# Issuing a four-layer graph kernel in the exact order of its own list schedule

## The chip, the cores and the metric

The kernel runs on one core of a Trainium2 chip. The metric is the device time of one execution in microseconds (us). Each number of a run below is the median of its timed executions.

The engines are called PE (TensorE, matrix products and transposes), ACT (ScalarE), DVE (VectorE), POOL (GpSimd) and SP (which issues the DMAs). L462 means line 462 of the kernel.

## The reference, cut to what matters

The input is x of 64 x 256 x 128 and one adjacency of 256 x 256, all in fp32. Four residual layers follow one another, each closed by a layer norm.

```python
x = _layernorm(x + gated_gnn(x, adj, 5 steps))      # layer 0
x = _layernorm(x + softmax_adjacency_gnn(x, adj))   # layer 1
x = _layernorm(x + gat_then_gin(x, adj))            # layer 2: two layer norms inside
x = _layernorm(x + chebyshev(adj, x, order 3))      # layer 3

# one step of layer 0 (u3, sigmoids, tanh: three gates in a row)
m  = adj @ h;  av = [m, m];  u3 = h @ u3_w.T + u3_b
z  = sigmoid(av @ w3_w.T + w3_b + u3)
r  = sigmoid(av @ w4_w.T + w4_b + u3)
hv = tanh(av @ w5_w.T + w5_b + (r * h @ u5_w.T + u5_b))
h  = (1 - z) * h + z * hv
```

The 64 batches are independent of one another. The kernel works on them as 32 pairs and keeps several pairs in flight, so that one pair's matmuls fill the time in which another pair waits.

## The kernel before

The kernel is written as a list of operations with what each reads and writes. A list scheduler in the kernel's own Python gives each operation a start time from assumed durations, chooses between ACT and DVE where both can do the work, and assigns the buffers. It then emits the instructions in order of these start times.

```python
SEEN = {"PE": 0.3, "ACT": 0.15, "DVE": 0.15, "POOL": 0.2, "SP": 3.3}   # handover to another engine
DUE, LAST_DUE, LAST = 50.0, 10.0, 7                                   # pace of the pairs, and of the last ones
...
    def order(self, tiles):
        ...
                for engine, us, fn in op.ways:
                    start = max(op.ready, held, engines[engine])
                    key = (start + (us if len(op.ways) > 1 else 0.0), self.due(op.pair) - op.rest, op.number)
                    if best is None or key < best[0]:
                        best = key, start, op, engine, us, fn
        ...
            out.append((start, op.number, op, fn))
        ...
        return [(op, fn) for _, _, op, fn in sorted(out, key=lambda x: x[:2])]
```

The layer norm: its statistics are on DVE, two small steps on POOL add epsilon and raise to the power of -0.5, a small DVE step (L462) makes the offset, and four instructions on ACT (L473) or DVE (L468) normalise.

```python
        dve(1.75, fn, [y], [st, s])                        # L455: 4 bn_stats (L452) and 4 bn_aggr (L454)
        ...
        pool(1.04, lambda: nc.gpsimd.tensor_tensor(rs(), rs(), neg_half.ap, op=ALU.pow), [s, neg_half], [s])   # L460
        nmr = lambda: s.at(32)[:, 12:16]
        dve(0.16, lambda: nc.vector.scalar_tensor_tensor(nmr(), mv()[:, :, 0], -1.0, rs(), op0=ALU.mult, op1=ALU.mult), [s], [s])   # L462
        ...
        S.add([("ACT", 1.85, by_act), ("DVE", 1.45, by_dve)], [y, s], [o])          # L475: L473 or L468
```

Layer 0, which is most of the matrix work, has three tanhs (ACT: L491, L497, L505) and four gate products (DVE: L493, L507, L508, L510) between its matmuls. In all but the last four pairs its state is turned by a DVE transpose (L421), a DMA to DRAM (L422) and four DMAs back (L426); this is so both before and after the change. PSUM tiles are copied out by ACT (L192) or DVE (L193).

The end of the kernel hands the list to the framework. The framework has a scheduler of its own, and before the change that scheduler was free to set the order of each engine's instructions.

```python
    for op, fn in S.order(tiles):
        for v, ap in op.tiles.items():
            v.ap = ap
        fn()
```

Of the kernel before, what the change touches and what calls it, by code (L numbers as in the profile page):

```python
# [165 lines left out]
def kernel(ctx: ExitStack, tc: tile.TileContext, x, xT, adj, adjT, mats, cols, rows, out):  # L166
# [6 lines left out]
    S = Schedule(n_pairs)  # L173
# [485 lines left out]
    tiles = {}  # L659
    for cls, (n, count) in CLASSES.items():  # L660
        where = {"PS": psum, "D": dram, "E": dram}.get(cls, shared)
        tiles[cls] = [where.tile([1, n] if cls == "D" else [P, n], F32, name=f"{cls.lower()}{k}") for k in range(count)]
    for op, fn in S.order(tiles):
        for v, ap in op.tiles.items():
            v.ap = ap
        fn()


# [39 lines left out]
```

## Time and profile before

The time on which the prediction was made was 1814.8 us, the median of three runs.

The prediction below shows the busy sums, the waits, PE's gaps, the time at half clock and how many instructions stood out of the list's order. Two more views help to see where in the execution the time was lost. First the windows of the kernel before. The columns are the window, its length, the busy us of PE, PE's weight loads, DVE, ACT and POOL with their instructions, the granted clock (as a share of full speed), the DMA share and GB/s.

```profile
0.00:1500.00 1500.00, 1417.83 (x5885) 1001.60 (x5886) 1010.86 (x2750) 710.22 (x1478) 341.19 (x397) 0.99 0.20 61
1500.00:1809.00 309.00, 267.54 (x1333) 204.45 (x1331) 200.49 (x712) 149.99 (x342) 99.17 (x122) 0.96 0.05 14
```

PE lacked 82 us of the first 1500 us, where many pairs are in flight. This is not a shortage of other pairs' work, and no other engine was full there: DVE was busy for two thirds of it. Next, the shares of the span in the chain of work that ended last.

```profile
PE 18%; DVE 11%; POOL 6%; ACT 3%; issue 2%; DMA 1%; SPq 0%; POOLq 0%; DVEq 0%; ACTq 0%
```

The shares sum to 41%: the profile could follow this chain back only to about 1049 us. In the part that it did follow, PE is less than half of the way, and small work on DVE and POOL takes nearly as much.

### The profile page before, as it was taken

How to read it: one execution, taken by the hardware profiler on the slowest of the kernel's cores; microseconds unless marked ns; L12 is line 12 of the kernel's file. 1: busy time of each engine (PE TensorE's matmuls, PEld its weight loads, DVE VectorE, ACT ScalarE, POOL GpSimd, SP SyncE). 2: the span in 40 equal slices, each digit the busy share in tenths (PEclk: the TensorE clock that was granted, in tenths of full speed). 3: DMA queues.
4: the chain of work that ended last, by engine and by line, in shares of the span. 5: the costliest groups of instructions: out<-in, count | busy, mean ns of one | idle time of the engine just before them, and what ended most of it. 6: DMA issues, size and time to landing. Idle time of an engine off the chain costs nothing. (4 is left out here: it accounts for less than half of the span.)

```text
span 1808.5 us, 22671 instructions
## 1 busy us (share of the span) xinstructions
PE 1685.4 (93%) x7216; PEld 1206.1 (67%) x7216; DVE 1211.3 (67%) x3461; ACT 860.2 (48%) x1820; POOL 440.4 (24%) x519
## 2 busy tenths in 40 slices
PE   8999999998999999999999999999999999998886
PEld 5666676667667667676675766667667666666765
DVE  5667666766766765767758576667657755767764
ACT  3444543455455453555444444435544634444653
POOL 0002221113322222212222113221322031215352
PEclk9999999999999999999999999999999999999899
DMA  6211112221111212211212121212211100000000
GB/s 191 92 60 59 41 53 65 87 65 35 59 41 52 84 37 63 88 47 48 70 36 73 44 77 42 70 36 70 76 35 48 59 24 7 7 18 7 12 24 24
DMA packets 129623, 96.13 MB, mean 53 GB/s; under 512 B 11872, under 2 KB 110688, under 8 KB 129504
## 3 DMA queue, kind: packets, MB, share of 16 engines
q1 hardware_dynamic: 129504, 94.69, 16.9%
q8 instruction: 57, 0.93, 0.2%
q14 instruction: 62, 0.51, 0.1%
HBM read 56.83 MB, written 37.81 MB: 52 GB/s over the span
## 5 line engine op out<-in xcount | busy, mean ns | idle before, releaser
L192 ACT COPY a<-ps 128x512 f32<-128x512 f32 (+1 forms) x422 | 215.3, 520 | 292.4 <-PE ps L438 189.5
L457 POOL TENSOR_SCALAR s<-s 128x4 f32<-128x4 f32 x160 | 53.5, 334 | 948.6 <-DVE s L454 853.6
L438 PEld LDWEIGHTS ps<-aT,a 128*128 128x128 f32 x1024 | 248.9, 309 | 33.6 <-issue 18.5
L438 PE MATMUL ps<-aT,a 128*128 128x256 f32 x1024 | 266.4, 401 | 1.4 <-ACT a L192 1.0
L460 POOL TENSOR_TENSOR s<-s,neg_half 128x4 f32<-128x4 f32 x192 | 202.1, 1053 | 15.8
L452 DVE BATCH_NORM_STATS2 s<-a 128x6 f32<-128x128 f32 x640 | 141.5, 281 | 60.5 <-ACT a L192 58.7
L505 ACT ACTIVATE a<-ps,bzrh 128x512 f32<-128x512 f32 x160 | 109.0, 682 | 142.9 <-PE ps L503 140.6
L462 DVE SCALAR_TENSOR_TENSOR s<-s 128x4 f32<-128x4 f32 x192 | 38.5, 201 | 206.3 <-POOL s L460 206.1
L491 ACT ACTIVATE a<-ps,bzrh 128x512 f32<-128x512 f32 x160 | 108.9, 682 | 136.9 <-PE ps L488 135.9
L503 PE MATMUL ps<-a,u5h 128*128 128x512 f32 x320 | 165.9, 600 | 8.0 <-DVE a L493 8.0
L495 PE MATMUL ps<-a,w 128*128 128x512 f32 x320 | 164.0, 603 | 9.4 <-ACT a L491 9.3
L488 PE MATMUL ps<-a,w 128*128 128x512 f32 x320 | 164.6, 597 | 5.6 <-ACT a L192 5.6
L502 PE MATMUL ps<-a,w 128*128 128x512 f32 x320 | 164.6, 596 | 0.0
L529 PEld LDWEIGHTS ps<-W,a 128*128 128x128 f32 x1024 | 128.1, 194 | 51.3 <-ACT a L192 19.9
L529 PE MATMUL ps<-W,a 128*128 128x128 f32 x1024 | 135.1, 280 | 24.1 <-ACT a L192 13.2
L473 ACT ACTIVATE x<-a,s 128x128 f32<-128x128 f32 x248 | 107.9, 485 | 97.3 <-DVE s L462 97.3
L507 DVE TENSOR_TENSOR a<-a,a 128x512 f32<-128x512 f32 x128 | 93.3, 729 | 72.1 <-ACT a L505 72.0
L493 DVE SCALAR_TENSOR_TENSOR a<-a,a 128x512 f32<-128x512 f32 x128 | 89.7, 703 | 64.7 <-ACT a L491 64.1
L487 PE MATMUL ps<-a,W 128*128 128x512 f32 x256 | 131.1, 594 | 1.4 <-DVE h L555 1.3
L508 DVE SCALAR_TENSOR_TENSOR a<-a,a 128x512 f32<-128x512 f32 x160 | 120.0, 752 | 18.1 <-ACT a L497 15.5
L497 ACT ACTIVATE a<-ps,bzrh 128x512 f32<-128x512 f32 x160 | 108.8, 682 | 47.9 <-PE ps L495 46.9
L438 PE MATMUL ps<-aT,x 128*128 128x256 f32 x512 | 128.4, 392 | 3.3 <-ACT x L473 3.2
(147 smaller groups left out, 2816.1 us busy)
## 6 DMA issues: line engine op xcount, KB each, us to landing
e<-a SPq DMA_DIRECT2D x112, 256.0 KB
a<-e SPq DMA_DIRECT2D x448, 64.0 KB
t<-xT_in SPq DMA_DIRECT2D x32, 256.0 KB
x<-x_in SPq DMA_DIRECT2D x32, 256.0 KB
a<-d SPq DMA_DIRECT2D x32, 256.0 KB
y_out<-a SPq DMA_DIRECT2D x32, 256.0 KB
W<-mats_in SPq DMA_DIRECT2D x1, 832.0 KB
W<-mats_in SPq DMA_DIRECT2D x1, 512.0 KB
```

Of the source, the lines that this page charges most:

```text
L192: S.add([("ACT", us_act, lambda: nc.scalar.copy(o(), i())), ("DVE", us_dve, lambda: nc.vector.tensor_copy(o(), i()))], r, w)
L438: nc.tensor.matmul(t.at(2, N)[:, b, :], i.tile(2 * b + j), right.ap[:, j, :], start=(j == 0), stop=(j == 1))
L452: nc.vector.bn_stats(st.at(4, 6)[:, c, :], tokens(y)[:, c, :])
L460: pool(1.04, lambda: nc.gpsimd.tensor_tensor(rs(), rs(), neg_half.ap, op=ALU.pow), [s, neg_half], [s])
L487: nc.tensor.matmul(t.at(512), mat("u3"), hT.at(512), start=True, stop=False)
L488: nc.tensor.matmul(t.at(512), w345.ap[:, 1, :], mT.at(512), start=False, stop=True)
L495: pe(mm(512), lambda t=t, mT=mT: nc.tensor.matmul(t.at(512), w345.ap[:, 0, :], mT.at(512), start=False, stop=True, skip_group_check=True), ...
L502: nc.tensor.matmul(t.at(512), w345.ap[:, 2, :], mT.at(512), start=True, stop=False)
L503: nc.tensor.matmul(t.at(512), u5h.ap, r.at(512), start=False, stop=True)
L505: act(0.69, lambda t=t, hv=hv: nc.scalar.activation(hv.at(512), t.at(512), AF.Tanh, bias=bzrh.ap[:, 2:3]), [t, bzrh], [hv])
L508: dve(0.74, lambda hv=hv, z=z: nc.vector.scalar_tensor_tensor(hv.at(512), z.at(512), 1.0, hv.at(512), op0=ALU.add, op1=ALU.mult), [hv, z], ...
L529: nc.tensor.matmul(tokens(t)[:, c, :], tokens(i)[:, c, :], w(), start=(k == 0), stop=(k == len(lefts) - 1))
```

## The change

The intent is to keep the list's order, which the kernel had computed with the handovers and buffers in view, through to the chip. The whole diff:

```diff
-    for op, fn in S.order(tiles):
-        for v, ap in op.tiles.items():
-            v.ap = ap
-        fn()
+    with tc.manual_schedule():
+        for op, fn in S.order(tiles):
+            for v, ap in op.tiles.items():
+                v.ap = ap
+            fn()
```

Inside this block every engine issues in program order. The instructions and the buffers are the same in both builds.

## The prediction

> **What bounds the kernel now.** I read the page's first two parts, the windows, the waits of TensorE, then those of ScalarE (ACT) and VectorE (DVE), and last the timeline around single gaps. The page says who is full:
>
> ```profile
> PE 1685.4 (93%) x7216; PEld 1206.1 (67%) x7216; DVE 1211.3 (67%) x3461; ACT 860.2 (48%) x1820; POOL 440.4 (24%) x519
> PEclk9999999999999999999999999999999999999899
> ```
>
> TensorE is the bound: 93% busy, with 1808.5 - 1685.4 = 123 us in which no matmul runs, 7 us of that after the last matmul. DVE and ACT have a third and a half of the span to spare, so their sums do not bound; only when they do things can. The windows, in four stretches of 400 us and one of 209, put PE at 382.6, 377.0, 373.3, 383.3 and 169.2 us busy: 84 us of the idle time lie before 1600 us, where many pairs of batches are in flight and there is plenty of other work, and about 40 in the tail, where few pairs are left. What PE waited for, the largest:
>
> ```profile
> PE ps L642 <- ACT a L192: 14.5, 7, 3.3
> PE ps L529 <- ACT a L192: 13.2, 10, 3.8
> PE ps L402 <- DVE a L510: 13.1, 6, 4.2
> PE ps L495 <- ACT a L491: 9.3, 10, 2.0
> PE ps L529 <- ACT a L612: 8.2, 8, 1.7
> PE ps L503 <- DVE a L493: 8.0, 5, 2.8
> ```
>
> So PE waits for short results, a PSUM copy (L192), a tanh (L491), a gate product (L493), from engines that are half idle. Why were these late? The columns are total us, times, longest us:
>
> ```profile
> DVE s L462 <- POOL s L460: 206.1, 178, 4.3
> ...
> ACT x L473 <- DVE s L462: 97.3, 49, 6.3
> ACT a L603 <- POOL a L602: 78.2, 24, 5.9
> ACT a L473 <- DVE s L462: 71.0, 37, 6.6
> ...
> ACT b L579 <- DVE s L571: 48.5, 24, 4.9
> ```
>
> These are layer-norm and softmax steps that stand in ACT's and DVE's queues before their inputs exist, most of them waiting for the 1.05 us power on POOL (L460, 192 times). One case from the timeline (start, duration, what, idle before and its releaser), ACT, then PE:
>
> ```profile
> 1142.49 0.37 ACT L192 COPY a<-ps 128x256 f32<-128x256 f32 x1 [1.04 <-PE ps L635]
> 1147.75 0.51 ACT L579 ACTIVATE b<-b,h 128x256 f32<-128x256 f32 x1 [4.89 <-DVE s L571]
> 1148.17 0.35 ACT L192 COPY a<-ps 128x256 f32<-128x256 f32 x1
> ...
> 1148.57 0.67 PE L642 MATMUL ps<-a,a2T 128*128 128x256 f32 x1 [3.02 <-ACT a L192]
> ```
>
> The L635 products were done by about 1144.2, but ACT sat 4.89 us at L579 with the copy behind it, and PE stood still 3.02 us. It then paid again; the windows of this gap and of what follows it (third column from the right: granted clock):
>
> ```profile
> 1145.50:1148.60 3.10, 0.08 (x2) 0.03 (x1) 2.18 (x6) 0.85 (x3) 0.89 (x1) 1.00 0.22 63
> 1148.70:1152.10 3.40, 3.40 (x9) 2.69 (x10) 2.90 (x12) 2.78 (x10) 0.00 (x0) 0.51 0.21 78
> ```
>
> For 3.4 us after the gap PE ran at half clock. The trace has 16 such stretches; by their lengths they cost 31 us (the mean granted clock, 0.983, gives the same: 0.017 x 1808.5). Of 19 gaps of 2 us or more, 13 are followed by one within 4 us.
>
> [...]
>
> **The change part by part.** No instruction is added or taken away: the builds have the same 4092 matmuls, 3461 DVE, 512 POOL and 726 DMA instructions, and buffers are given out by the list before emission, so they are the same too. Only the place of each instruction in its engine's queue changes. In the old build 43 of 4092 PE instructions stand out of the list's order, against 841 of 3461 on DVE and 472 of 1689 on ACT (least number to move to restore it); in the new build none do. The move of each instruction, counted as the trace duration of the work placed ahead of it on its engine:
> - ACT: the normalisations L473 go later in 373 of 472 cases, 3.9 us on average; L603 in 23 of 25, 3.8 us. What feeds PE goes earlier: the three tanhs in 333 of 480 cases, by some 1.9 us, the copies L192 in 250 of 423, by 1.35 us.
> - DVE: L468 (normalisation) goes later in 240 of 296, L565 in 56 of 64 (3.2 us), L571 in 27 of 32 (3.0 us); L508, L510, L588 and the statistics go earlier, by 0.7, 0.8, 2.2 and 1.4 us.
> - PE and SP keep nearly all places, and 142 of 192 POOL powers keep theirs.
>
> In the case above the old queue has the first L579 ahead of three L192 copies; the new one has it behind them.
>
> The cost, step by step. (1) I paired the trace with the built program and followed each PE gap (95 over 0.03 us, 115.8 us, the 6.1 us of the first load included) back to the first instruction that started over 0.15 us after its inputs, and looked at what ran ahead of it there. In 80 gaps, 94.4 us, something that ran ahead stands behind it in the new order: 58.8 us on ACT, 35.6 on DVE; 77 of the 94 lie before 1600 us. I let 80% go, -75 us. (2) New waits: a fixed order still misses where the list's durations are off. Its POOL, DVE and ACT durations are close to the trace (power 1.04 against 1.053, transpose 1.11 against 1.114, four statistics with aggregation 1.75 against 4 x 0.281 + 4 x 0.158 = 1.756), its transposes through PE less so. I choose +15 us. (3) PE idle thus goes from 116 to some 56 us. Long gaps should fall at least as much: half clock from 31 to some 15 us, -16 us. (4) Steps between matmuls that are over 0.1 us above the median of their kind sum to 171 us; gaps and clock account for 116 + 31 less the 2 us of half clock after the last matmul, leaving some 25 us of refill after a stall. Fewer stalls: -10 us. Sum -75 + 15 - 16 - 10 = -86, so 1814.8 - 86 = 1729; I round to 1727.
>
> A floor for comparison: the median steps between matmuls sum to 1607.6 us; with 6 us ahead of the first matmul, 7 us after the last and the 6 us between profile and timing, 1627. The range stays well above it.
>
> **The rivals.** (a) *The stall moves, it does not go.* Strict order makes ACT and DVE issue whole groups: the statistics of one tile hold DVE 1.75 us where the old build could slip a gate product in between. If the list misjudges DMA or PE, the head of a queue blocks as before. For it: 5 of 64 L565 go earlier and 42 of 160 L493 later. Against: L493 is on average earlier, and a turned state lands a median 7.8 us before PE first reads it, with only 0.4 us of PE waits put down to those transfers. It would give 1775 to 1810. (b) *The tail decides.* After 1600 us the chain runs through POOL powers and DVE reductions, and order cannot shorten a dependence. Then only the part before 1600 us is won, about 60 us with its clock: 1755. (c) *Everything the list plans comes true*: idle some 25 us and hardly any half clock, 1690. (d) *DMA or the two half-idle engines become the bound*: the sums, 1211 us DVE and 17% of the DMA queues, speak against it; no time goes to it.
>
> **Range and chances.** Rival (c) is the low end, a weak form of (a) the high end: 1690 to 1770. Faster by over 2% needs under 1778.5, that is only 36 us of the 86. Since 80 of 95 gaps have their blocker moved, I give that 0.92; within 2% 0.06; slower 0.02, for an order that blocks in ways which the old trace cannot show.
>
> **What would show it right or wrong.** Right: PE busy share of 96% or more; the waits of L473, L603 and L579 on ACT (97.3 + 71.0 + 78.2 + 48.5 = 295 us) at least halved, that of L462 on POOL well down; PE waits on L192, L491 and L493 down to a third; granted clock above 0.99; PE, DVE and ACT busy sums unchanged within 2%, apart from PE's at half clock. Wrong, if PE's idle time stays above 90 us with new lines at the head of its waits (DMA a<-e, L588 or L421), or if the ACT waits fall and the span does not, which would make the tail or PE's own pitch the bound.

## The result

The changed kernel took 1691.38 us (1689.64 to 1693.74, four runs). In the same rounds the kernel before took 1815.44 us (1813.13 to 1819.7, four runs). The ratio is 0.9315, with a 95% interval from 0.9294 to 0.9336. A ratio here is the mean time of one kernel's runs over that of the other's of the same rounds, so it is not quite the ratio of the medians. The change is 124 us faster; the time predicted was 1727 and the range 1690 to 1770, so the result lies 1.4 us inside its lower end.

The busy sums of the kernel after:

```profile
PE 1646.8 (97%) x7216; PEld 1198.1 (71%) x7216; DVE 1257.4 (74%) x3461; ACT 875.1 (52%) x1820; POOL 451.8 (27%) x519
```

PE's idle time fell from 123 to 1689.5 - 1646.8 = 43 us. Its busy time also fell by 38.6 us with the same instructions: some 19 us of this is less time at half clock, and the rest, as the account below suggests, is fewer slow matmuls around a stall. Now the windows of the kernel after, in the same columns as above (the second one ends with the span, at 1689.5 us).

```profile
0.00:1500.00 1500.00, 1489.92 (x6350) 1069.12 (x6351) 1121.72 (x2970) 772.31 (x1569) 373.36 (x424) 1.00 0.20 62
1500.00:1809.00 309.00, 156.84 (x869) 129.00 (x866) 135.68 (x491) 102.83 (x251) 78.44 (x95) 0.96 0.04 11
```

Of the first 1500 us PE now lacks 10, and 8.3 of those are the wait for the first load. PE got through 6350 instead of 5885 instructions in that time. After 1500 us it lacks 189.5 - 156.8 = 33 us: what is left of the idle time is in the tail.

The waits of PE after (total us, times, longest us), largest first:

```profile
PE ps L438 <- DMA aT<-adjT_in: 8.3, 1, 8.3
PE ps L305 <- ACT b L582: 6.8, 4, 6.1
PE ps L438 <- ACT x L473: 3.3, 2, 3.1
PE ps L529 <- ACT a L612: 2.6, 3, 0.9
```

The copies, tanhs and gate products that led this list before are gone from its head. The second line is new: L305, the transposes of the softmax, waited 1.1 us for L582 before. The account of the prediction comes back to it. The waits on L192 copies fell from 41.7 to 5.2 us in all, those on L491 from 9.3 to 0.8, and those on L493 from 8.0 to nothing. The waits of ACT and DVE after, which answer to the lines of L462, L473, L603 and L579 before:

```profile
ACT a L192 <- PE ps L438: 225.0, 196, 10.1
...
DVE s L462 <- POOL s L460: 43.5, 52, 2.4
...
ACT b L579 <- DVE s L571: 9.7, 13, 1.7
...
ACT a L603 <- POOL a L602: 5.1, 9, 1.2
...
ACT a L473 <- DVE s L462: 3.0, 2, 1.7
ACT x L473 <- DVE s L462: 3.0, 2, 2.2
```

ACT is still idle for half of the span, but now it waits almost only for PE, that is, for the bound: 763 of the 804 us of its waits, against 619 of 939 us before. The waits of L473 (both tiles), L603 and L579 together went from 295 to 3.0 + 3.0 + 5.1 + 9.7 = 21 us. The chain that ended last, after:

```profile
PE 93%; DVE 3%; ACT 1%; POOL 1%; issue 1%; DMA 0%; SPq 0%; POOLq 0%; DVEq 0%; ACTq 0%
```

The prediction showed a case in which ACT stood 4.89 us at an L579 with a ready copy behind it. The same place in the list comes at about 1064 us of the kernel after. First ACT in its timeline (start, duration, what, idle before and its releaser), then PE:

```profile
1063.76 0.37 ACT L192 COPY a<-ps 128x256 f32<-128x256 f32 x1 [1.43 <-PE ps L642]
1064.62 0.37 ACT L192 COPY a<-ps 128x256 f32<-128x256 f32 x1 [0.49 <-PE ps L642]
1065.55 0.59 ACT L192 COPY a<-ps 128x512 f32<-128x512 f32 x1 [0.56 <-PE ps L438]
...
1062.69 1.89 PE L642 MATMUL ps<-a,a2T 128*128 128x256 f32 x8
1064.42 1.10 PE L438 MATMUL ps<-aT,a 128*128 128x256 f32 x4
```

The copies come first, each a little after its product, and the activations follow at 1066.03 us, when their input has long been there. PE has no idle time at all, where before it stood still for 3.02 us at this L642 and then ran 3.4 us at half clock.

The account of the two traces, in us:

| | before | after | difference |
|---|---|---|---|
| start, up to the first matmul | 6.1 | 8.3 | +2.2 |
| PE gaps up to 1500 us | 76.0 (63 gaps) | 1.8 (3 gaps) | -74.2 |
| PE gaps after 1500 us | 33.7 | 25.0 | -8.7 |
| half clock, up to the last matmul | 29.0 | 10.2 | -18.8 |
| refill: long steps beyond gaps and clock | 31.9 | 14.1 | -17.8 |
| steps up to 0.1 us above their median | 17.7 | 15.8 | -1.9 |
| sum | | | -119.2 |

The sum agrees with the spans (1689.5 - 1808.5 = -119.0). The fourth row is the time by which the stretches at half clock were longer than at full clock; there were 16 of them before and 4 after, of which one each lay after the last matmul and is not in this row. The fifth row takes all steps between matmuls over 0.1 us above the median of their kind (170.6 us before, 51.1 after) and takes off the gaps after the first matmul and the clock.

### The profile page after: what moved, and what is told of

The parts are those of the page before. It is cut to its first block, busy times and chain, and to the rows that moved or that the text cites.

```text
span 1689.5 us, 22635 instructions
## 1 busy us (share of the span) xinstructions
PE 1646.8 (97%) x7216; PEld 1198.1 (71%) x7216; DVE 1257.4 (74%) x3461; ACT 875.1 (52%) x1820; POOL 451.8 (27%) x519
## 4 chain that ended last, share of the span: by engine, by line
PE 93%; DVE 3%; ACT 1%; POOL 1%; issue 1%; DMA 0%; SPq 0%; POOLq 0%; DVEq 0%; ACTq 0%
PE ps L438 26%; PE ps L495 8%; PE ps L487 8%; PE ps L488 8%; PE ps L502 8%; PE ps L503 8%; PE ps L529 6%; PE ps L402 4%; PE ps L596 3%; PE ps L634 3%; PE ps L635 3%; PE ps L642 3%; PE ps L553 2%; PE ps L305 2%; POOL s L460 1%
## 5 line engine op out<-in xcount | busy, mean ns | idle before, releaser
L192 ACT COPY a<-ps 128x512 f32<-128x512 f32 (+1 forms) x422 | 218.4, 525 | 359.1 <-PE ps L438 225.0
L438 PEld LDWEIGHTS ps<-aT,a 128*128 128x128 f32 x1024 | 248.1, 309 | 30.5 <-issue 18.2
L438 PE MATMUL ps<-aT,a 128*128 128x256 f32 x1024 | 264.5, 399 | 0.7 <-ACT a L192 0.7
L460 POOL TENSOR_TENSOR s<-s,neg_half 128x4 f32<-128x4 f32 x192 | 214.0, 1115 | 15.8
L491 ACT ACTIVATE a<-ps,bzrh 128x512 f32<-128x512 f32 x160 | 109.7, 687 | 173.9 <-PE ps L488 170.5
L502 PE MATMUL ps<-a,w 128*128 128x512 f32 x320 | 163.5, 592 | 0.0
L452 DVE BATCH_NORM_STATS2 s<-a 128x6 f32<-128x128 f32 x640 | 140.3, 280 | 31.2 <-ACT a L192 27.6
L488 PE MATMUL ps<-a,w 128*128 128x512 f32 x320 | 163.4, 592 | 0.0
L495 PE MATMUL ps<-a,w 128*128 128x512 f32 x320 | 160.7, 593 | 0.8 <-ACT a L491 0.8
L507 DVE TENSOR_TENSOR a<-a,a 128x512 f32<-128x512 f32 x128 | 92.1, 720 | 74.3 <-ACT a L505 74.2
L438 PE MATMUL ps<-aT,x 128*128 128x256 f32 x512 | 126.3, 388 | 11.6 <-DMA aT<-adjT_in 8.3
L493 DVE SCALAR_TENSOR_TENSOR a<-a,a 128x512 f32<-128x512 f32 x128 | 91.7, 719 | 57.3 <-ACT a L491 56.6
L529 PE MATMUL ps<-W,a 128*128 128x128 f32 x1024 | 129.7, 276 | 4.2 <-ACT a L612 2.6
L421 DVE STREAM_TRANSPOSE a<-a 128x512 f32<-128x512 f32 x112 | 124.8, 1120 | 2.8
L438 PEld LDWEIGHTS ps<-aT,x 128*128 128x128 f32 x512 | 97.8, 195 | 40.6 <-issue 16.0
```

The source lines that it names most:

```text
L192: S.add([("ACT", us_act, lambda: nc.scalar.copy(o(), i())), ("DVE", us_dve, lambda: nc.vector.tensor_copy(o(), i()))], r, w)
L421: dve(1.11, lambda: nc.vector.transpose(st.ap.rearrange("p (b l t) -> p t b l", b=4, l=32), i.blocks()), [i], [st])
L438: nc.tensor.matmul(t.at(2, N)[:, b, :], i.tile(2 * b + j), right.ap[:, j, :], start=(j == 0), stop=(j == 1))
L452: nc.vector.bn_stats(st.at(4, 6)[:, c, :], tokens(y)[:, c, :])
L488: nc.tensor.matmul(t.at(512), w345.ap[:, 1, :], mT.at(512), start=False, stop=True)
L495: pe(mm(512), lambda t=t, mT=mT: nc.tensor.matmul(t.at(512), w345.ap[:, 0, :], mT.at(512), start=False, stop=True, skip_group_check=True), ...
```

## The experiments

The theory: what waits at the head of an engine's queue holds what stands behind it, as ACT held a ready copy for 4.89 us at L579 in the trace before. The framework's order puts steps whose input is not there early, above all L462 behind the POOL power, and what PE needs stands behind them. Rivals are that PE's, POOL's or the DMAs' order carries the gain, that the power's latency itself is the loss, and that the gain comes from a good plan rather than from keeping to one. Each group of runs had its own timings of the kernel before: 1812.48 us for e1 to e4, 1813.92 for e5 to e8, and 1814.05 for e9 to e12. The results are correct unless I say so.

### Which engine's order counts: e1 to e4

The framework takes a set of engines that keep the program's order; the others stay free.

```diff
-    with tc.manual_schedule():
+    with tc.manual_schedule(engines={mybir.EngineType.Activation}):     # e1; e2: DVE; e3: both; e4: PE, Pool, SP
```

**e1, ACT alone.**

> Only ACT issues in the list's order (no ACT instruction out of place, DVE 831, PE 31). Theory (blocked heads of both ACT's and DVE's queues made PE wait, ACT the larger part: 58.8 of the 94.4 us of PE gaps whose blocker was moved): about 1735 us, some 60 to 70% of the gain of 124 us; the ACT waits of L473, L603 and L579 fall well below half of 295 us, the DVE wait of L462 on POOL stays near 206 us. Rival 1 (order of PE, POOL and SP matters): stays above 1790. Rival 2 (DVE's order is the root, ACT only hands its delays on): stays above 1790. Rival 3 (either queue alone is enough): under 1710.

Measured: 1742.66 us, ratio 0.962 [0.9586, 0.9653]. ACT's waits of L473, L603 and L579 fell to some 13 us, but in the waits of DVE the line of L462 stood as before:

```profile
DVE s L462 <- POOL s L460: 205.9, 178, 3.5
```

Some 70 us are won, 56% of 124 and a little under the 60 to 70% expected. PE's gaps were 71 us.

**e2, DVE alone.**

> Only DVE issues in the list's order (DVE 0 out of place, ACT 331, PE 43). Theory: about 1765 us, 35 to 45% of the gain; the DVE wait of L462 on POOL falls to some 45 us as in the kernel after, the ACT waits of L473, L603 and L579 stay above 150 us and PE keeps its waits for L192 and L491. Rival 2 (DVE is the root): under 1710. Rival 1: stays above 1790.

Measured: 1699.82 us, ratio 0.9378 [0.9358, 0.9397]. The expectation was missed by some 65 us: I had given DVE's order the smaller share. It wins 113 us, 91% of the whole. Its lines of the waits of DVE and ACT:

```profile
DVE s L462 <- POOL s L460: 40.8, 52, 2.1
...
ACT a L603 <- POOL a L602: 53.8, 25, 4.5
```

ACT is still held for 147 us at L473, L603 and L579 in all, half as long as before, with 331 of its instructions out of the list's order. Yet PE's gaps are only 39 us. So a long wait of a queue is not by itself a loss.

**e3, ACT and DVE.**

> ACT and DVE both in the list's order, PE, POOL and SP free (PE 31, POOL 7, SP 29 out of place). Theory: within 5 us of the kernel after, 1686 to 1697 us. Rival 1 (PE, POOL or SP order carries part of it): at least 15 us slower than the kernel after.

Measured: 1688.28 us, ratio 0.9315 [0.9298, 0.9332], the same ratio as the whole change has.

**e4, PE, POOL and SP.**

> PE, POOL and SP in the list's order, ACT and DVE free (ACT 466, DVE 846 out of place). Theory: within 1% of the kernel before, 1800 to 1825 us, with ACT and DVE waits as before. Rival 1: under 1780 us.

Measured: 1826.53 us, ratio 1.0086 [1.006, 1.0111]: 0.9% slower than before, and 1.5 us above the expected range. Its waits of ACT and DVE stayed as before (L462 at 196 us).

What follows: the gain lies in the order on DVE and ACT and nowhere else. The two shares overlap, 70 + 113 being more than 124; that one engine's late result lengthens the other's wait is the likely reason, and e5 to e7 bear on it. The rival that PE, POOL or the DMA queue carries it falls.

### Which displaced instructions count: e5 to e7

These runs start from the changed kernel, with every engine in exact order, and put chosen steps early in the list, as the framework had done. The differences below are taken from the changed kernel's 1691.38 us, which was timed in another group of rounds; by the ratios they come out within 2 us of the same. In e5 it is L462, right behind its POOL power; in e6 the normalisations L473 and L468, right behind L462; in e7 both. The engines and buffers are those of the changed kernel.

```diff
-            out.append((start, op.number, op, fn))
+            op.issue = max([b.issue for b in op.before] + [issued.get(id(v.ap), 0.0) for v in op.writes]) + 1e-6 if op.early else start
+            ...                                      # issued: the latest place at which each tile was used
+            out.append((op.issue, op.number, op, fn))
...
-        dve(0.16, lambda: nc.vector.scalar_tensor_tensor(nmr(), ...
+        dve(0.16, lambda: nc.vector.scalar_tensor_tensor(nmr(), ...; S.ops[-1].early = True          # e5, e7
...
-        S.add([("ACT", 1.85, by_act), ("DVE", 1.45, by_dve)], [y, s], [o])
+        S.add([("ACT", 1.85, by_act), ("DVE", 1.45, by_dve)], [y, s], [o]); S.ops[-1].early = True   # e6, e7
```

Two theories stood against each other: that the early L462 is the root by itself, or that the early normalisations are.

**e5, L462 early.** In the build, 159 of its 192 instances move ahead of a mean 1.65 us of DVE's work.

> The kernel after, with one thing moved: each L462 (DVE, 4 elements per partition) is issued right behind its POOL power in the list, so that it stands on average 1.65 us of DVE work earlier in DVE's queue (159 of 192 moved); PE, ACT, POOL and SP keep their order. Theory T1 (what hurts is DVE's head blocked on POOL): the DVE wait of L462 rises from 43 to 150 to 220 us and the time to 1720 to 1750 us, near the run with only ACT in order. Theory T2 (what hurts is bulk normalisation work ahead of the work that feeds PE): under 1702 us.

Measured: 1706.27 us, ratio 0.9405 [0.9377, 0.9432]. Its line in the waits of DVE:

```profile
DVE s L462 <- POOL s L460: 179.2, 181, 2.5
```

The wait grew from 43.5 to 179.2 us, and the time by only 1706.27 - 1691.38 = 15 us. Both theories missed, the first by far. The wait that led the list of DVE before is thus largely harmless as long as the rest stands in order.

**e6, the normalisations early.** They move ahead of some 4.6 (ACT) and 8.0 us (DVE) of work, which puts copies, tanhs and gates 1.0 to 1.5 us later.

> The kernel after, with only the normalisations (L473 on ACT, L468 on DVE) moved up to right behind their L462 in the list: L473 4.6 us and L468 8.0 us of work earlier on average, which puts the copies, tanhs and gate products 1.0 to 1.5 us later; the waits for POOL stay as they are (L462 about 43 us). Theory T1: under 1705 us. Theory T2: 1725 us or more, with PE waiting for L192, L491 and L493 again.

Measured: 1726.87 us, ratio 0.9512 [0.9479, 0.9545], that is 35 us above the changed kernel. PE's gaps are 59 us, while L462 waits only 33 us. The second theory's size came true, but it accounts for less than a third of the 124.

**e7, both early.**

> The kernel after with both moved up: L462 behind its power and the normalisations behind L462. This imitates on purpose what the framework did. T1 and T2 together: 1740 to 1790 us, with L462's wait above 150 us and ACT's waits of L473 above 60 us. If either move alone explains all, this is within 10 us of that one.

Measured: 1794.03 us, ratio 0.9886 [0.9857, 0.9916], just above the 1740 to 1790 that I had expected. Its lines in the waits of ACT, then of PE:

```profile
ACT x L473 <- DVE s L462: 97.0, 54, 5.5
...
PE ps L529 <- ACT a L192: 17.3, 10, 3.1
```

Two displacements that cost 15 and 35 us alone cost 103 together. The trace of e7 shows the chain: L462 stands at the head of DVE's queue for its power and delays what DVE owes others; L473, early in ACT's queue, waits for that L462 (97.0 us on x, 97.3 before); and copies, tanhs and gates for PE stand behind both. The run also shows that the loss comes from the order and not from something else that the block does, for the block is in place here.

That e7 is near the kernel before in time, and in PE's gaps (111 against 115.8 us), is in part chance. PE's instructions stand in the same order in the kernel after and in e5 to e7, so their traces can be compared by work: the time up to the start of the 6351st of PE's 7216 instructions, and from there to the end (in the kernel before, PE's order is nearly the same).

| us | before | after | e5 | e6 | e7 |
|---|---|---|---|---|---|
| first 6350 PE instructions | 1613.1 | 1500.1 | 1507.2 | 1512.0 | 1568.9 |
| the rest | 195.4 | 189.4 | 199.0 | 214.1 | 220.7 |

In the steady part, where the change won 113 us, the two displacements cost 7 and 12 us alone and 69 together, 61% of it. The other 31 us of e7, like most of e6's loss, lie in the tail, where the kernel before was only 6 us slower than the one after. So some 44 us of the steady part would be due to other displaced steps, such as L603, whose wait stays at 4.7 us here (78.2 before); that is argued, not shown.

### Is it the power's latency or its place: e8 and e9

These two give a wrong result (relative error 441). The two POOL steps of each layer norm become one DVE step that needs no POOL. e8 is the kernel before with this edit and e9 the kernel after.

```diff
-        ... the epsilon step on POOL (L456 to L459)
-        pool(1.04, lambda: nc.gpsimd.tensor_tensor(rs(), rs(), neg_half.ap, op=ALU.pow), [s, neg_half], [s])
+        dve(0.16, lambda: nc.vector.tensor_scalar(rs(), mv()[:, :, 1], 0.0, 0.7, op0=ALU.mult, op1=ALU.add), [s], [s])
```

> Wrong result on purpose: the kernel before (the framework's own order), with the two POOL steps of each layer norm replaced by one DVE instruction that writes a constant scale, so that nothing waits for a POOL power. DVE stays out of the list's order (846 instructions), ACT too (407). T1: at least 60% of the gain comes without any change of order, under 1740 us, and L462 waits for nothing. T2: above 1770 us, since normalisations still stand too early.

> Wrong result on purpose, control for the run before: the kernel after (exact order) with the two POOL steps of each layer norm replaced by one DVE instruction. If the 119 us that the same removal won in the framework's order came from queues blocked behind the POOL power, the exact order, where little is blocked, wins little by it: 1675 to 1692 us. If they came from the shorter layer-norm chain itself, it wins again some 60 us or more: under 1635 us, against the floor of 1627.

Measured: e8 1694.73 us, ratio 0.9342 [0.9314, 0.937]; e9 1677.86 us, ratio 0.925 [0.9225, 0.9275]. In the framework's order (DVE 846 and ACT 407 instructions out of the list's order, about as before) the POOL steps were worth 1813.92 - 1694.73 = 119 us. In exact order the same steps are worth 1691.38 - 1677.86 = 14 us (12 by the two ratios). So their own latency costs little; the other 105 us before were paid by what stood behind it in two queues. The rival that latency itself was the loss falls. Without the POOL steps the framework's order costs only 1694.73 - 1677.86 = 17 us, so it does little harm when these long waits are not in it.

### Does the plan or the keeping to it count: e10 to e12

**e10** sets the list's durations to about the steps from start to start that the trace shows where an engine has work without idle time, and lengthens the handovers of ACT and DVE.

```diff
-SEEN = {"PE": 0.3, "ACT": 0.15, "DVE": 0.15, "POOL": 0.2, "SP": 3.3}
+SEEN = {"PE": 0.3, "ACT": 0.25, "DVE": 0.25, "POOL": 0.2, "SP": 3.3}
-        dve(1.75, fn, [y], [st, s])
+        dve(1.17, fn, [y], [st, s])
-        S.add([("ACT", 1.85, by_act), ("DVE", 1.45, by_dve)], [y, s], [o])
+        S.add([("ACT", 1.56, by_act), ("DVE", 1.2, by_dve)], [y, s], [o])
...                                                     # and some twenty more of this kind
```

> The kernel after with the list's durations set to the steps between starts that the trace of after shows (512-wide DVE 0.61 in place of 0.70 to 0.76, four statistics with aggregation 1.17 for 1.75, tanh 0.59 for 0.69, four normalisations on ACT 1.56 for 1.85 and so on, the handover of ACT and DVE 0.25 for 0.15); all else equal. Before 1500 us the kernel after has hardly a gap, so only the tail can win: 1675 to 1692 us. If the wrong durations still cost something in the steady part, under 1670.

Measured: 1694.27 us, ratio 0.9339 [0.932, 0.9359]. The interval overlaps that of the change, so better durations alone won nothing that shows. It was expected at 1675 to 1692 us, so this run was a miss as an improvement.

**e11** adds what the tail and the start asked for: the adjacency and the first x are loaded first, the last 16 pairs instead of 7 are paced more closely, and the last four pairs are turned by DVE and DMA too.

```diff
-BY_PE = 4
+BY_PE = 0
-DUE, LAST_DUE, LAST = 50.0, 10.0, 7
+DUE, LAST_DUE, LAST = 50.0, 6.0, 16
-    load_x(0)
     load(lambda: aT.ap, adjT.rearrange("(t p) i -> p t i", p=P), aT)
+    load_x(0, True)                                    # True: x ahead of its transpose
...                                                     # durations as in e10, transposes 0.44
```

> The same durations, and for the ends of the run: adjacency and the tokens of the first pair loaded first, the due dates of the last 16 pairs 6 us apart in place of the last 7 at 10 us, and all states turned by DVE and DMA (no pair left to PE transposes). Exact order. The trace of after has some 27 us of PE gaps, 10 us of half clock and 14 us of refill after its first matmul, nearly all after 1500 us, and 8.3 us before it; taking off half of that and 3 us of the start: 1655 to 1675 us, the fastest of all. If the tail is bound by the dependences of the last pairs, it stays above 1685.

Measured: 1660.67 us (1659.59 to 1662.37), ratio 0.9154 [0.9133, 0.9175]. It beats both kernels: 8.5% below the kernel before and, by the two ratios, 0.9154 / 0.9315 = 0.983, some 1.7% below the change. Its busy sums:

```profile
PE 1633.9 (98%) x7152; PEld 1193.3 (72%) x7152; DVE 1260.0 (76%) x3495; ACT 854.9 (51%) x1786; POOL 454.4 (27%) x519
```

PE's gaps are 19 us, of which 7.6 are the start, and half clock appears only after the last matmul. The 64 fewer PE instructions are the transposes of the last four pairs. Which of the three edits carries the gain was not tried.

**e12** is e11 without the exact order: the block around the loop is taken away.

```diff
-    with tc.manual_schedule():
+    if True:
```

> The same as the run before it, but without the manual schedule: the framework orders the instructions (DVE 654, ACT 376, PE 14 out of the list's order). If the exact order is what the gain hangs on whatever the plan, this is 70 to 130 us slower than that run; if a better plan makes the framework's freedom harmless, within 25 us of it.

Measured: 1800.69 us, ratio 0.9927 [0.9907, 0.9946]. With 654 DVE and 376 ACT instructions out of order again, the better plan is 140 us slower than e11, somewhat more than the 70 to 130 us expected. In its waits of DVE the old line is back (L463 and L461 are L462 and L460, one line lower):

```profile
DVE s L463 <- POOL s L461: 205.7, 167, 3.1
```

So the better plan is worth 1814.05 - 1800.69 = 13 us when the framework may reorder it, while keeping to the order is worth 124 us under the first plan and 140 under the better one. Why the framework puts L462 so early was not tried and stays open.

## Why the prediction was right or wrong

The direction and the mechanism were right: a gap of PE was mostly a late copy, tanh or gate, behind a step of DVE or ACT that waited at the head of its queue. The time fell in the range, but only 1.4 us inside its lower end, where rival (c), that everything the list plans comes true, had put it at 1690. The number of that rival came nearest, though not its working: it had some 25 us of PE idle time, and 43 us were measured. The prediction's own sum of 86 us was too small by 33 us (the span fell by 119), and its terms say where.

- **Step 1, "I let 80% go, -75 us", and step 2, "+15 us" of new waits.** Together -60 us; measured 115.8 to 35.1, that is -80.7. This term was the most mis-sized. Step 2 was too large and looked in the wrong place. Up to 1500 us only three gaps of 1.8 us in all remain after the start, although the list's durations are off: it counts the four statistics with their aggregation as 1.75 us, the sum of the durations in the trace, while the step from their start to the next instruction's is about 1.07 (median of those without idle time), since such instructions overlap. Why this does so little harm stays open. That such reserves in the plan absorb errors is a guess, and e10, which took many of them away (1.17 for 1.75) but lengthened the handovers, still had gaps of only 5.3 us up to 1500 us.
- **A new wait did come, in the tail.** It is the longest gap of PE after the first load, 6.1 of the 35.1 us. DVE, ACT and PE there:

```profile
1560.89 1.21 DVE L571 TENSOR_REDUCE s<-b 128x4 f32<-128x1024 f32 x1
...
1566.46 0.13 DVE L574 TENSOR_TENSOR s<-s,h 128x4 f32<-128x4 f32 x1
...
1567.09 0.51 ACT L582 ACTIVATE b<-b,s 128x256 f32<-128x256 f32 x1 [3.26 <-DVE s L576]
...
1567.74 2.38 PE L305 MATMUL ps<-ident,b 128*128 128x128 f32 x8 [6.09 <-ACT b L582]
```

Between L571 and the small softmax steps L574 to L576, DVE worked through adds and three groups of layer-norm statistics without a pause (L616, L452, L454, L617), and PE stood. From 1563.1 to 1576.7 us it was also at half clock, which cost 6.8 us. So here the list's own order holds PE up.
- **The split of step 1, 58.8 us on ACT and 35.6 on DVE.** This was not a split of the gain. e1 won 70 and e2 113 us. Following each gap to the first late instruction finds the last queue in the chain, which need not be the one where the delay began: with L462 late on DVE, L473 waits on ACT, and the gap is then put down to ACT.
- **Step 3, half clock -16 us.** Measured -19.2 with what lies after the last matmul (31.2 to 12.0). Right.
- **Step 4, refill -10 us.** Measured -17.8. It was mis-sized at its base: the working took the 6.1 us before the first matmul off a sum of steps between matmuls that does not hold them, so "some 25 us of refill" was 31.9. The fall itself was also larger, in line with the gaps.
- **The start** was not in the sum and cost 2.2 us: the first matmul is now an L438 that waits for the adjacency. The floor of 1627 also took 6 us between profile and timing; the profiled execution shows 1.8 (1810.28 - 1808.5).
- **Rival (a)**, that the stall moves, came about once, as shown above, and not in the steady part; the lines that the prediction named as its signs (DMA a<-e, L588, L421) are not at the head. **Rival (b)**, the tail, was right as far as it went: after 1500 us only 8.7 us of gaps were won. But a tail that is planned better gets shorter when the order is kept: PE's gaps after 1500 us are 2.9 us in e11 and 32.7 us in e12, which has the same plan. **Rival (d)** fell: the DMA share of the steady part is 0.20 in both.
- **The checks.** PE at 97%, the ACT waits far below half, L462 down, the PE waits on L192, L491 and L493 below a third, and the clock at 0.993 all came true. One failed: the busy sums of DVE and ACT were to stay within 2%, and DVE's rose by 3.8%, from 1211.3 to 1257.4 (ACT's by 1.7%).

The last point has two parts. Busy time counts overlapping records once. The durations of DVE's instructions, added up one by one, rose by only 1.4% (1443.0 to 1462.7 us). The other 26 us is overlap between one instruction and the next, which fell from 231.7 to 205.3 us. And of the 20 us of longer durations, 19 are at L468, the normalisation on DVE, whose durations went from 110.6 to 129.5 us in all. The groups of its largest form, before and then after (count, busy us, mean ns, idle):

```profile
L468 DVE TENSOR_SCALAR x<-a,s 128x128 f32<-128x128 f32 x136 | 42.6, 356 | 0.4
```

```profile
L468 DVE TENSOR_SCALAR x<-a,s 128x128 f32<-128x128 f32 x136 | 54.2, 468 | 0.0
```

Single instances took 0.88 to 1.45 us: 23 after and 5 before. Every one ran beside a 128x512 instruction on POOL (L538, L601, L602 or L605) and ended 0.08 to 0.09 us after such an instruction ended. Without such company none took over 0.46 us. Nor was every meeting slow: of the instances that ran beside one of these four, 33 of 38 before and 34 of 57 after stayed under 0.46 us too. What ties the two engines together was not shown. The slow instances hold PE up at one place in the kernel after, as its timelines of DVE, POOL and PE show:

```profile
1538.58 4.19 DVE L468 TENSOR_SCALAR x<-a,s 128x128 f32<-128x128 f32 x4
...
1539.83 1.26 POOL L601 TENSOR_TENSOR a<-a,rbc 128x512 f32<-128x512 f32 x1
1541.17 1.26 POOL L602 TENSOR_TENSOR a<-a,rbc 128x512 f32<-128x512 f32 x1
...
1541.23 0.33 PE L402 MATMUL ps<-ident,x 128*128 128x128 f32 x1 [0.98 <-DVE x L468]
1542.57 0.73 PE L402 MATMUL ps<-ident,x 128*128 128x128 f32 x2 [1.01 <-DVE x L468]
```

Four normalisations took 4.19 us instead of about 1.4 (4 x 0.35), PE stood twice for about 1 us, and a stretch at half clock followed from 1542.6 us. The list does not know of such meetings, so it cannot keep away from them; that the higher count after is chance is argued, not shown.

## What to carry to other kernels

If a kernel plans its own order with durations, handovers and buffers, check in the build whether each engine really issues in that order before tuning the plan. A step that waited at the head of DVE's queue was harmless or costly by what stood behind it (the early L462 cost 15 us alone in e5 and was part of 103 us in e7), so try displacements together as well as alone. To find the root of PE's gaps, follow the chain of waits past the first late instruction, and hold one engine's order at a time.

## What the traces show of the clock, the power and the waits

- Before, a gap of 2.0 us at 1084.1 us was already followed by 3.41 us at half clock, and 13 of the 19 gaps of 2 us or more were followed by half clock within 4 us. After, two gaps of 0.98 and 1.01 us with short matmuls between were enough (PE busy 0.66 of the 3.0 us from 1539.5 us on). The half-clock stretches of each trace lie on one grid of 3.413 us. Counted over all 14 traces in windows of that grid at full clock, from the first clock record on (12.1 us before, 13.4 us after), each of the 71 windows with PE busy below 0.42 was followed by half clock (14 of them in the trace before, 4 in the trace after), of those above 0.56 none was, and in between some were.
- A power on POOL at 128x4 took 1.053 us in the mean of 192 before and 1.115 us after, against 0.334 and 0.344 us for an add of the same size.
- The total of a wait was no measure of its cost: L462's 179 us of waits cost 15 us in e5, and 160 us of the same waits, with the normalisations early too, were part of a loss of 103 us in e7.
